# Scores of four heads in one group in the last steps of a causal attention

## The chip, the cores and the metric

The kernel runs on one core of one Trainium2 chip. The metric is the device time of one execution in microseconds (us), the median over several runs. A profiled execution was taken beside them; its rows are what the text quotes.

## The reference

Three blocks in a row: a half-weighted mixture-of-experts layer, an attention, and the same expert layer again, each on layer-normalised rows. x has 4 sequences of 2048 rows with 256 columns. Cut to the attention, which alone is touched (16 heads of 16 columns):

```python
q = (x @ Wq)...; k = (x @ Wk)...; v = (x @ Wv)...
node_probs = jax.nn.softmax((x @ Wr)..., axis=-1)
...
q_r = q * cos_w + rotate_half(q) * sin_w
k_r = k * cos_w + rotate_half(k) * sin_w
node_w = jnp.einsum('bhik,bhjk->bhij', node_probs, node_probs)
scores = jnp.einsum('bhid,bhjd->bhij', q_r, k_r) * SCALE
scores = scores + jnp.log(node_w + 1e-08)
scores = jnp.where(causal[None, None], scores, -jnp.inf)
attn = jax.nn.softmax(scores, axis=-1)
out = jnp.einsum('bhij,bhjd->bhid', attn, v)
return out.transpose(0, 2, 1, 3).reshape(B, S, E) @ Wo
```

## The kernel before

**Three stages.** `experts` runs twice, before and after `attention`, each with its own pools of SBUF and PSUM. The second call begins when the pools of the attention have been given back.

**Units and steps.** The attention works on units: one sequence and one group of four heads, 16 units in all. Within a unit the queries are cut into four blocks of 512 (`ib`), and for each block the keys are gone through in pieces of 128 rows (`at`, listed in `turns`). One such piece is a step: 36 in a unit, 576 in all. A step is 512 queries wide; the pieces on the diagonal are packed, so that the step "two" consists of a piece of 384 and one of 128 columns, and the step "one" is 256 wide. Each head occupies one strip of 32 partitions of the tiles qT and kT, so a matmul of one head uses one 32-row strip of the TensorE array.

**What a step does.** For each head, `scores` (L1037) multiplies a kT piece with the qT block into one PSUM bank; `weights` takes exp of it on ScalarE into an SBUF tile `ex`, and on masked pieces GpSimd cuts off what lies above the diagonal; `summed` (L1063) multiplies ex with the values into the accumulators acc[0] and acc[1] (one for each half of the four nodes), and `summed_weights` (L1080) into den.

**Maxima.** The scores of a block need the maximum of each query row first. `maximum` (L1104) computes the scores the other way round, queries by keys, for two heads into two PSUM banks, and VectorE reduces them. When all of a block are there, `negated` turns them (a ps_t transpose, L1130) and adds them to qT. This work is kept in two lists, `left[0]` and `left[1]` (one for each pair of heads), and `take` issues one entry. The maxima run ahead of the steps that need them: `ask` issues those of the very first block at once, and during the first unit the loop takes additional ones. So the lists run out before the steps do.

**The order of instructions** is written out by hand in `run`: nothing reorders the queues. For each step it goes through two phases, `pair` 0 and 1. A phase issues the scores of the *next* step for one pair of heads, one entry of maxima for the other pair of heads (`take(1 - pair, width)`), the exps of that pair of the next step, and then one half of the sums of the current step. So while maxima are left, two scores and two maxima, on four different strips, stand one after the other on TensorE; afterwards the two scores stand there alone. Behind each phase side work is put in: generators for preparing the next unit, for `normalise` (ps_o transposes, L1146) and `project` (ps_p transposes, L1192; ScalarE copy to oc; ps_w matmuls, L1202). At the last step of a block ScalarE also copies acc[0] (after phase 0), acc[1] and den (after phase 1) out of PSUM.

**PSUM.** Of the eight banks, acc[0], acc[1] and den hold three. `bank(name, tag)` hands out the others in two rings: tag "sc" with two banks, for scores, and tag "mx" with three, for maxima and for all side work (ps_o, ps_p, ps_w, ps_t).

```python
BANKS = {"sc": 2, "mx": 3}
...
return ps_rg.tile([P, 512], F32, name=name, tag=tag, bufs=BANKS[tag])
```

All operations of VectorE, ScalarE and GpSimd in the attention pass through a recording helper, so the profile shows them under its line, L78. Names tell them apart: ex<-sc is the exp of a score, top<-mx the reduction of a maximum. TensorE's weight loads are listed as an engine of their own, PEld. An fp32 matmul leaves two records.

Of the kernel before, what the change touches and what calls it, by code (L numbers as in the profile page):

```python
# [94 lines left out]
def macaron_kernel(  # L95
# [487 lines left out]
    def attention():  # L583
# [43 lines left out]
        def bank(name, tag="mx"):  # L627
            if not gaps["steps"]:
                tag = turn_of.pop(0)
                turn_of.append(tag)  # L630
            return ps_rg.tile([P, 512], F32, name=name, tag=tag, bufs=BANKS[tag])
# [374 lines left out]
        def pieces(ib, at):  # L1006
            if at == "two":
                return [(4 * ib + 1, P, 3 * P, 0), (4 * ib + 3, 3 * P, P, 3 * P)]
            if at == "one":
                return [(4 * ib + 2, 2 * P, 2 * P, 0)]  # L1010
            return [(at, 0, 512, 0)]

        def columns(at):
            return 256 if at == "one" else 512
# [10 lines left out]
                return t[:, of[0] : of[0] + P].unsqueeze(1)  # L1025
            return t.rearrange("p (n w) -> p n w", w=P)[:, of[0] // P : of[1] // P + 1 : 3, :]

        def scores(u, ib, at, pair):

            q = u["qT"][ib]  # L1030
            out = [bank("sc", "sc") for _ in range(2)]
            for jt, off, n, to in pieces(ib, at):
                k = u["kT"][jt // 4]
                js = slice((jt % 4) * P, (jt % 4 + 1) * P)
                for j in range(2):
                    r = slice(32 * (2 * pair + j), 32 * (2 * pair + j) + 32)
                    nc.tensor.matmul(  # L1037
                        out[j][:, to : to + n], lhsT=k[r, js], rhs=q[r, off : off + n],
                        start=True, stop=True,
                    )  # L1040
            return out

        def weights(tiles, u, ib, at, pair):
            n = columns(at)
            for j in range(2):
                ex = pool.tile([P, 512], F32, name="ex", tag="ex", bufs=8)
                act.activation(ex[:, 0:n], tiles[j][:, 0:n], AF.Exp, scale=D**-0.5)
                cut = masked(ib, at)
                if cut:
                    diag = blocks(ex, cut)  # L1050
                    gps.affine_select(
                        out=diag, in_=diag, pattern=[[0, len(cut)], [1, P]],
                        compare_op=ALU.is_ge, fill=0.0, base=0, channel_multiplier=-1,
                    )
                u["ex"][2 * pair + j] = ex
# [168 lines left out]
        def maxima(ib):  # L1224

            wide = [(i, c) for c in range(ib) for i in range(4)]
            heavy = ["two", (3, ib)]
            if not wide:
                return [(at, at) for at in heavy[:1] + ["one"] + heavy[1:]]
            order = [o for at, w in zip(heavy, (0, 2)) for o in ((at, wide[w]), (wide[w], at))]  # L1230
            order += [(wide[1], wide[1]), (wide[3], wide[3])]
            return order + [("one", "one")] + [(at, at) for at in wide[4:]]

        left = {
            pair: [(u, ib, at) for u in units for ib in range(NI) for at in maxima(ib)]
            for pair in range(2)
        }
# [98 lines left out]
        def begin(phase):  # L1336
            nonlocal begun
            if begun < len(units):
                w = units[begun]
                behind.append(prepare(w))  # L1340
                due.append([phase, STEPS[w["g"] == 0], w])
                begun += 1
# [9 lines left out]
        def onward(force=False):  # L1352

            w = due[0]
            took = advance(behind, force)
            parted()
            if not took and [g.__name__ for g in behind[:2]] == ["quarter"] * 2:
                took = advance(behind, False, 1)
            w[1] -= took is True
            if w[2]["ready"]:  # L1360
                due.pop(0)
            return took

        def pace(phase):

            if due:
                for _ in range(max(1, -(-due[0][1] // max(1, due[0][0] - phase)))):
                    if not due or not onward(phase > due[0][0]):
                        break
# [4 lines left out]
        while units[0]["blocks"] < NI:  # L1374
# [6 lines left out]
            at = min(some, key=lambda at: max(known.get(id(behind[at]), (0, [0.0]))[1]))  # L1381
# [7 lines left out]
        def order(u, behind):  # L1389

            while u["shared"] and u["queued"] < min(NI, 1 + behind):
                urgent.append(weighted(u, 4 * u["queued"]))
                u["queued"] += 1

        def run():
            for n, (u, ib, at) in enumerate(steps):
                if n == 0:
                    begin(span // 2)
                if ib == NI - 1 and at == turns[ib][0]:

                    begin(2 * n + span - 8)
                if n == 0:
                    for pair in range(2):
                        weights(scores(u, ib, at, pair), u, ib, at, pair)
                ex = dict(u["ex"])
                order(u, NI)
                while len(u["vn"]) <= max(jt for jt, _, _, _ in pieces(ib, at)) // 4:
                    advance(urgent, True)
                nxt = steps[n + 1] if n + 1 < len(steps) else None
                width = columns(nxt[2]) if nxt is not None else 512  # L1410
                if nxt is not None and nxt[2] == turns[nxt[1]][0]:
                    while nxt[0]["blocks"] <= nxt[1]:
                        onward(True)
                    ask(nxt[0], nxt[1])
                last = at == turns[ib][-1]
                for pair in range(2):
                    gaps["free"] = True
                    clock.now = max(clock.now, vec.end - LAG, act.end - LAG)
                    clock.now += 1.07 * width / 512
                    if nxt is not None:  # L1420
                        made = scores(*nxt, pair)
                    take(1 - pair, width)
                    if u is units[0] and ib > 0 and n % 2 and pair:
                        take(0)
                        take(1)
                    if nxt is not None:
                        weights(made, *nxt, pair)
                    summed(u, ib, at, pair, ex)
                    summed_weights(u, ib, at, ex, pair)
                    clock.now += 1.5 * columns(at) / 512  # L1430
                    if pair == 0:
                        if last:
                            while held:
                                advance(urgent, True)
                            got = [
                                pool.tile([P, 512], F32, name="oT", tag="oT", bufs=3)
                                for _ in range(3)
                            ]
                            act.copy(got[0], acc[0])
                        pass  # L1440
                    else:
                        if last:
                            act.copy(got[1], acc[1])
                            act.copy(got[2], den)
                            if u["g"] == 0:
                                outs[u["b"], ib] = pool.tile([P, 4, E], F32, name="o", tag="o", bufs=5)
                            held.append((id(u), ib))
                            urgent.append(normalise(u, ib, got))
                            if u["g"] == NG - 1:
                                urgent.append(project(u["b"], ib))  # L1450
                    if pair == 1 and ib == NI - 1:
                        after = units.index(u) + 1
                        if after < len(units):
                            order(units[after], sum(
                                turns[ib].index(at) >= max(
                                    m for m, o in enumerate(turns[ib])
                                    if any(jt // 4 == b for jt, _, _, _ in pieces(ib, o))
                                )
                                for b in range(NI)
                            ))  # L1460
                    if not advance(first):
                        advance(urgent)
                    pace(2 * n + pair)
            gaps["free"] = True
            while advance(urgent, True):
                pass

        with tc.manual_schedule():
            run()
# [45 lines left out]
```

## Time and profile before

| What | us |
|---|---|
| Median of 3 timed runs | 4581.84 |
| Lowest and highest of them | 4573.15, 4585.91 |
| Profiled execution | 4589.68 |
| Span of its records | 4588.0 |
| Mean granted TensorE clock | 0.932 |
| First expert stage and start of the attention, 0 to 700: TensorE busy | 471.82 |
| Attention, 3800 to 4000: TensorE busy | 198.20 of 200.00 |
| Attention without maxima, 4066.15 to 4160.15: TensorE busy | 94.00 of 94.00 |
| End of the attention, 4160.15 to 4182.78: TensorE busy | 10.46 of 22.63 |
| Second expert stage, 4182.78 to 4588.0: TensorE busy | 252.36 of 405.22 |

How to read the profile: one execution on the chip, times in microseconds from the start of the span. Each row names the engine, the line of the kernel, the operation, and the tiles as out<-in, with partitions x elements. Matmuls are pipelined and their ends are modelled, so two rows on TensorE may overlap; the distance from the start of one group to the start of the next is the better measure of what a group costs. In a row of the timeline, the number after the opening bracket is the engine's idle time before it, and behind the arrow stands what ended it.

### The profile page before, as it was taken

The page shows a single profiled execution, that of the slowest core. Times are in us where ns is not written, and L with a number is a line of the kernel's source. Part 1 is how long each engine was busy: PE and PEld are TensorE (multiplying, and loading weights), DVE is VectorE, ACT ScalarE, POOL GpSimd, SP SyncE. Part 2 cuts the span into 40 slices and gives each one's busy share as a digit, 9 for nine tenths or more (in the row PEclk, how much of TensorE's full clock was granted, in tenths as well). Part 3 has the DMA queues.
Part 4 walks back from the last instruction along what each step waited for, and adds up shares of the span by engine and source line. Part 5 has one row for each costly group of instructions (what it writes and reads, how often), then busy time and mean ns, then how long its engine had stood idle before and what let it go on. Part 6 is the DMA issues. An engine that isn't in the chain of part 4 may idle for free. (4 is left out here: it accounts for less than half of the span.)

```text
span 4588.0 us, 89695 instructions
## 1 busy us (share of the span) xinstructions
PE 4118.6 (90%) x36512; PEld 1841.0 (40%) x36512; DVE 2957.4 (64%) x7855; ACT 1907.3 (42%) x3671; POOL 1644.3 (36%) x2482
## 2 busy tenths in 40 slices
PE   5575598999999999999989999999999999997376
PEld 2354333434344434443434443444444444332254
DVE  6852666667755667676667776767576767523771
ACT  4133132444454445455434454454344444444122
POOL 4285322243324333342233342413242424202177
PEclk8686688999999999999999999999999999998588
DMA  7244000000000000001000000010000000004144
GB/s 251 66 81 89 1 1 1 1 1 1 20 29 20 17 13 1 1 1 38 15 15 29 1 1 1 1 38 15 29 15 1 1 1 2 1 29 147 60 73 75
DMA packets 108046, 136.27 MB, mean 30 GB/s; under 512 B 7792, under 2 KB 102256, under 8 KB 106480
## 3 DMA queue, kind: packets, MB, share of 16 engines
q1 hardware_dynamic: 81152, 95.84, 6.4%
q0 software_dynamic: 24576, 33.57, 4.5%
q8 instruction: 286, 4.69, 0.4%
q10 hardware_dynamic: 1904, 1.13, 0.1%
q14 instruction: 128, 1.05, 0.1%
HBM read 77.03 MB, written 61.87 MB: 30 GB/s over the span
## 5 line engine op out<-in xcount | busy, mean ns | idle before, releaser
L78 ACT ACTIVATE ex<-sc 128x512 f32<-128x512 f32 (+1 forms) x2304 | 1197.7, 572 | 1579.5 <-PE mx L1104 1342.1
L1104 PE MATMUL mx<-kT,qT 32*128 32x512 f32 (+3 forms) x5120 | 1355.1, 581 | 10.3 <-DVE top L78 9.6
L78 DVE TENSOR_REDUCE top<-mx 128x1 f32<-128x512 f32 x1536 | 1003.1, 684 | 490.5 <-PE mx L1104 485.5
L1037 PE MATMUL sc<-qT,kT 32*128 32x512 f32 (+3 forms) x5120 | 1297.3, 576 | 12.8 <-ACT ex L78 9.2
L1063 PE MATMUL acc<-ex,vn 128*32 128x512 f32 (+3 forms) x10240 | 1188.7, 544 | 0.0
L78 POOL TENSOR_SCALAR_AFFINE_SELECT ex<-ex 128x128 f32<-128x128 f32 (+1 forms) x768 | 255.3, 338 | 1348.2 <-ACT ex L78 1337.9
L78 DVE CUSTOM_DVE_ANT_0 mx<-mx,edge 128x384 f32<-128x384 f32 (+3 forms) x1024 | 498.9, 503 | 315.5 <-PE mx L1104 248.9
L1080 PE MATMUL den<-ex,share 128*4 128x256 f32 (+1 forms) x9216 | 677.9, 370 | 0.0
L1037 PEld LDWEIGHTS sc<-qT,kT 32*128 32x128 f32 x5120 | 430.2, 185 | 417.3 <-ACT ex L78 216.1
L1063 PEld LDWEIGHTS acc<-ex,vn 128*32 128x32 f32 x10240 | 216.4, 108 | 778.0 <-issue 708.2
L1104 PEld LDWEIGHTS mx<-kT,qT 32*128 32x128 f32 x5120 | 452.5, 187 | 84.2 <-DVE top L78 73.7
L1080 PEld LDWEIGHTS den<-ex,share 128*4 128x4 f32 x9216 | 248.7, 88 | 579.4 <-issue 551.3
L78 POOL TENSOR_TENSOR by_node<-by_node 128x512 f32<-128x512 f32 x64 | 86.3, 1349 | 555.1 <-DVE by_node L78 555.0
L439 DVE TENSOR_SCALAR at<-row_b,low_t 128x128 bf16<-128x128 bf16 x1024 | 174.4, 286 | 57.0 <-PE ps_l L442 57.0
L482 POOL DMA_INDIRECT xg<-normed,where x128 | 130.2, 1017 | 207.0 <-DVE sc L461 168.6
L78 POOL TENSOR_TENSOR vn<-v,share 128x1024 f32<-128x1024 f32 x64 | 125.9, 1973 | 194.2 <-PE acc L1063 192.8
L501 ACT COPY xT<-ps_t 128x512 f32<-128x512 f32 x64 | 37.5, 586 | 303.0 <-PE ps_t L498 302.8
L530 PE MATMUL ps_o<-w,hT 128*128 128x256 f32 x512 | 147.3, 448 | 0.0
L78 DVE DVE_READ_ACCUMULATOR2_ANT top<- 128x1 f32 x1024 | 144.9, 141 | 0.0
L724 PEld LDWEIGHTS ps_a<-wa,xnT 128*128 128x128 f32 x1024 | 127.2, 202 | 27.5 <-issue 14.1
L724 PE MATMUL ps_a<-wa,xnT 128*128 128x80 f32 x1024 | 136.7, 289 | 0.0
L78 DVE TENSOR_TENSOR by_node<-ps_o,tot 128x512 f32<-128x512 f32 x128 | 88.0, 690 | 74.8 <-PE ps_o L1146 61.6
(218 smaller groups left out, 4788.8 us busy)
## 6 DMA issues: line engine op xcount, KB each, us to landing
xs<-x SPq DMA_DIRECT2D x32, 512.0 KB, 5.6
normed<-xn SPq DMA_DIRECT2D x32, 512.0 KB, 3.3
xs<-x SPq DMA_DIRECT2D x64, 256.0 KB, 2.7
w<-w SPq DMA_DIRECT2D x4, 2048.0 KB, 9.6
xs_o<-x SPq DMA_DIRECT2D x16, 512.0 KB, 3.9
x<-xs_o SPq DMA_DIRECT2D x16, 512.0 KB, 3.0
out<-xs_o SPq DMA_DIRECT2D x16, 512.0 KB, 4.1
xg<-normed,where POOLq DMA_INDIRECT x128, 2.7
```

What stands on the lines that cost most here:

```text
L78: return getattr(self.engine, name)(*args, **kw)
L439: nc.vector.tensor_scalar(at[:, t, :], row_b, low_t[:, c + t, e : e + 1], None, ALU.is_equal)
L482: inst = nc.gpsimd.indirect_dma_start(out=xg, out_offset=None, in_=normed, in_offset=bass.IndirectOffsetOnAxis(ap=lists[e][0][:, i : i + 1 ...
L501: nc.scalar.copy(xT[:, :, i * P : (i + 2) * P], ps)
L530: nc.tensor.matmul(po[:, j, :], lhsT=hT[:, f, at : at + P], rhs=w2[:, f, e, :], start=f == 0, stop=f == 1,)
L724: nc.tensor.matmul(ps[:, j, :], lhsT=u["xnT"][:, c, (t + j) * P : (t + j + 1) * P], rhs=wa[:, c, u["g"], cols], start=c == 0, stop=c == 1,)
L1037: nc.tensor.matmul(out[j][:, to : to + n], lhsT=k[r, js], rhs=q[r, off : off + n], start=True, stop=True,)
L1063: nc.tensor.matmul(acc[half][32 * h : 32 * h + 32, off : off + n], lhsT=u["vn"][jt // 4][:, jt % 4, h, 32 * half : 32 * half + 32], rhs=ex ...
L1080: nc.tensor.matmul(den[32 * h : 32 * h + K, off + a - to : off + z - to], lhsT=u["share"][:, jt, h, :], rhs=ex[h][:, a:z], start=at == tur ...
L1104: nc.tensor.matmul(made[j][:, to : to + n], lhsT=q[r, i * P : (i + 1) * P], rhs=u["kT"][c][r, 0:n], start=True, stop=True,)
```

## The change

In the steps in which no maximum is left in either list, the scores of both pairs of the next step are issued together in phase 0, four heads in a row; the third and fourth get banks of the ring "mx". The exps stay where they were: those of the first pair in phase 0, those of the second in phase 1. As long as maxima are left, nothing is changed.

```diff
-        def scores(u, ib, at, pair):
+        def scores(u, ib, at, *pairs):
 
             q = u["qT"][ib]
-            out = [bank("sc", "sc") for _ in range(2)]
+            heads = [2 * pair + j for pair in pairs for j in range(2)]
+            out = [bank("sc", tag) for tag in ("sc", "mx")[: len(pairs)] for _ in range(2)]
             for jt, off, n, to in pieces(ib, at):
                 k = u["kT"][jt // 4]
                 js = slice((jt % 4) * P, (jt % 4 + 1) * P)
-                for j in range(2):
-                    r = slice(32 * (2 * pair + j), 32 * (2 * pair + j) + 32)
+                for j, h in enumerate(heads):
+                    r = slice(32 * h, 32 * h + 32)
                     nc.tensor.matmul(
...
                 last = at == turns[ib][-1]
+
+                four = nxt is not None and not any(left.values())
                 for pair in range(2):
                     gaps["free"] = True
                     clock.now = max(clock.now, vec.end - LAG, act.end - LAG)
                     clock.now += 1.07 * width / 512
-                    if nxt is not None:
+                    if four and pair == 0:
+                        made = scores(*nxt, 0, 1)
+                    elif four:
+                        made = made[2:]
+                    elif nxt is not None:
                         made = scores(*nxt, pair)
                     take(1 - pair, width)
```

## The prediction

> **What bounds the kernel now.** First the page: which engine is full, and where.
>
> ```profile
> PE 4118.6 (90%) x36512; PEld 1841.0 (40%) x36512; DVE 2957.4 (64%) x7855; ACT 1907.3 (42%) x3671; POOL 1644.3 (36%) x2482
> PE   5575598999999999999989999999999999997376
> PEclk8686688999999999999999999999999999998588
> ```
>
> TensorE is 90% busy, and full in all of attention (slices 8 to 36 of 40; one slice is 114.7 us). At its busiest there is no other engine to blame: what shortens PE's work there shortens the run. Next the share of each engine in windows near the end of attention (columns: window, length, then busy us of PE, PEld, DVE, ACT, POOL, granted clock, DMA share, GB/s).
>
> ```profile
> 3800.00:4000.00 200.00, 198.20 (x2004) 73.33 (x1995) 136.20 (x322) 86.05 (x166) 69.55 (x121) 1.00 0.01 2
> 4066.15:4160.15 94.00, 94.00 (x772) 33.52 (x772) 6.02 (x13) 38.32 (x74) 7.07 (x18) 1.00 0.11 35
> ```
>
> The second window is the stretch without maxima: the last maximum matmul starts at 4064.2 by the rows of tile mx, and VectorE falls from 68% to 6%. PE stays at 94.00 of 94.00 at a granted clock of 1.00, ACT is busy 38.32. So PE bounds this stretch too, and only this stretch is edited. Third, the order of time on PE on both sides of that border (start, length, engine, line, operation):
>
> ```profile
> 4055.57 0.70 PE L1037 MATMUL sc<-qT,kT 32*128 32x512 f32 x2
> 4055.59 0.70 PE L1104 MATMUL mx<-kT,qT 32*128 32x512 f32 x2
> 4056.11 0.59 PE L1037 MATMUL sc<-qT,kT 32*128 32x512 f32 x2
> 4056.12 0.59 PE L1104 MATMUL mx<-kT,qT 32*128 32x512 f32 x2
> 4056.64 1.07 PE L1063 MATMUL acc<-ex,vn 128*32 128x512 f32 x8
> 4057.53 0.61 PE L1080 MATMUL den<-ex,share 128*4 128x256 f32 x8
> 4058.07 0.70 PE L1037 MATMUL sc<-qT,kT 32*128 32x512 f32 x2
> ...
> 4066.15 1.13 PE L1037 MATMUL sc<-qT,kT 32*128 32x512 f32 x4
> 4067.21 1.06 PE L1063 MATMUL acc<-ex,vn 128*32 128x512 f32 x8
> 4068.09 0.61 PE L1080 MATMUL den<-ex,share 128*4 128x256 f32 x8
> 4068.64 1.13 PE L1037 MATMUL sc<-qT,kT 32*128 32x512 f32 x4
> ```
>
> Each fp32 matmul leaves two records, so "x4" is two heads. Above the dots, two scores and two maxima, which use the other two 32-row strips of the array, run from 4055.57 to 4056.64: 1.07 us for four. Below, two scores alone run from 4066.15 to 4067.21: 1.06 us for two. A pair costs what four cost. acc then takes 0.88 (4067.21 to 4068.09), den 0.55; a phase is 2.49, a step of two phases 4.98.
>
> **The change, part by part.** In the changed program's PE order, the two score pairs of 17 steps have become one group of four, put where the first pair stood; no other instruction moves on PE, and the orders on DVE, ACT, POOL and SP are the same. The 17 are 14 steps of 512 columns, one in two pieces (384 and 128) and two of 256, all of the steps that start after 4066.15.
>
> Removed: 17 separate second pairs. A 512-wide pair is 1.06; the two-piece pair lasts from 4116.78 to 4117.84, 1.06; a 256-wide one from 4071.71 to 4072.34, 0.63. If the group of four costs what a pair costs, 15 x 1.06 + 2 x 0.63 = 17.2 us leave PE. How long four scores in a row last, no row shows: two of them always stood alone or beside maxima. Bounds: 1.06 (all strips at once) to 2.12 (one pair after the other, which is no gain). I take 1.06, because the row of two scores and two maxima has the same shape, the same four strips and four PSUM banks, and differs only in which operand is stationary.
>
> The Trainium skill, page "TensorE: Matmul & The Clock Gate", section "Measured speedup vs the span model", speaks against so full a gain: it lists four row tiles of K=32, N=512 at 3.07 times, not 4. By it, as an estimate, the group would last 4/3.07 = 1.30 pairs and the run would gain about 11 us instead. The trace's 1.07 against 1.06 does not agree with that figure, and the measurement decides.
>
> Added: waits for PSUM. Heads 3 and 4 now sit in the three mx banks until their exps are done, and these stand in ACT's queue behind whatever was put there between the phases. One ordinary step after the change is 1.06 + 2 x (0.88 + 0.55) = 3.92 us on PE. ACT begins 0.10 after the group's end (4101.75 to 4101.85) and takes 0.54 for an exp (1.08 for two): all four end at 1.06 + 0.10 + 2.16 = 3.32, so every bank is free 0.60 us before the next group wants it. VectorE, idle 94% here, frees the ps_o, ps_w and ps_t tiles that share the mx banks within a phase. The cover is ACT's slack; it is gone at three places, where a copy stands between the exps:
>
> ```profile
> 4079.81 1.36 PE L1037 MATMUL sc<-qT,kT 32*128 32x512 f32 x4
> 4081.66 1.56 PE L1037 MATMUL sc<-qT,kT 32*128 32x512 f32 x4
> ...
> 4084.58 0.65 PE L1192 MATMUL ps_p<-cst,o 128*128 128x128 f32 x4
> 4085.27 0.59 ACT L78 COPY oc<-ps_p 128x512 f32<-128x512 f32 x1 [1.26 <-PE ps_p L1192]
> ```
>
> (a) Twice a ps_p transpose (L1192) comes after the first phase, and its ACT copy waits for it: 1.06 + 1.43 + 0.59 + 0.10 + 0.59 = 3.77, then two exps to 4.85. PE, which also did the 0.59 of ps_p, wants the banks at 4.51. With 0.08 for the release (an estimate: the exps that end at 4082.05 and the scores behind them, done at 4083.15, leave 0.04 beyond 1.06): 0.42 each, 0.84 for both. Behind the waiting score stands all of PE's queue. (b) Once, where ib goes from 2 to 3, the step is short (256 columns: 1.06 + 0.45 + 0.55 + 0.45 = 2.51 on PE) and the copy of acc[0] (0.59) stands between the exps; the third ends at 1.06 + 0.10 + 1.08 + 0.59 + 0.54 = 3.37, with the release 3.45: a wait of 0.94. Together 1.78. In the rows above the kernel already waits there: 4079.81 to 4081.09 is 0.22 over 1.06, 4081.66 to 4083.15 is 0.43 over, together 0.65, which goes. Net added: 1.1, between -0.65 (no wait left) and, if each wait is twice that, 2.9.
>
> Sum: 17.2 - 1.1 = 16.1 us off the stretch of 94.00.
>
> What lies behind it moves up whole: the last normalise and project run from 4160.15, the last output transfer is issued at 4178.57, and VectorE's first instruction of the second expert stage starts at 4182.78, put down to that transfer; the loads of xs start at 4182.71. Nothing of that stage runs earlier, so no cover is lost and no queue other than PE's changes. Clock grants in that stage (mean 0.77) may fall otherwise by a few us either way; that is in the spread below.
>
> The profiled span 4588.0 (its run: 4589.68) becomes 4571.9. The profiled run is 0.17% above the median of the timed runs, 4581.84; the same 16.1 off the median gives 4565.7.
>
> **Rivals.**
> 1. *Four scores stretch each other.* All four read the same kT tile as weights and the same qT tile as moving data, where the maxima swap the two. For: no row shows four in a row. Against: a pair that shares both tiles lasts no longer than two scores and two maxima that don't. Midway between its bounds (1.59 a group) 8 of the 17 us stay: 4582 - 17.2/2 + 1.1 = 4574. The page named above would have it here, on this side of the middle.
> 2. *They don't overlap at all* (or the group waits each time about as long as a pair lasts): 4582 to 4583.
> 3. *Slower: the mx banks come back late in every step.* The place is the third and fourth score of each group, whose banks are held by the exps behind ACT's queue. It decides from a wait of 1.06 per step on, that is, with the last exp ending 4.98 after the group began, not 3.32. With 1.5 us in each, 17 x 1.5 - 17.2 = 8 us are lost: 4590. For: three banks for two heads and all side work, and a copy in the queue has this effect at three places. Against: ACT is busy 38.32 of 94.00, and sits idle 1.40 us before each ordinary pair of exps. The Trainium skill, page "TensorEngine Tiling (Array Packing)", section "PSUM Bottleneck", warns of just this: tiling quickens TensorE but not the emptying of PSUM. The trace agrees in kind only at the three places counted.
> 4. *The change does not act*: excluded but for its size, by the 17 groups in the order.
>
> **How the numbers follow.** Forecast 0.82, rival 1 0.07, rival 2 0.06, rival 3 0.05. The likeliest gives 4565.7. What a measurement here can tell from no change is about 0.3%, 13.7 us (the three runs lie 12.8 apart). The forecast clears that by little: I give it 9 in 10. Faster: 0.82 x 0.9 + 0.01 of rival 1 = 0.75; same: 0.08 + 0.06 + 0.06 = 0.20; slower 0.05. Range: the forecast's own bounds are gains of 17.8 (no wait left) and 14.3 (doubled waits), 4564 to 4567.5; a median of few runs may lie off by about half of those 12.8; and rival 1 belongs in. 4554 to 4580 leaves out part of the scatter, rival 2's upper half and rival 3.
>
> **What would show it.** In the profile after, PE's groups "sc x8" (four heads) should last 1.06 to 1.1 at 512 columns, be followed by acc, den, acc, den without scores between, every 3.9 us; the stretch without maxima should last 77 to 79 us; the waits of 0.4, 0.4 and 0.9 should stand before or inside the scores that follow the two ps_p copies and the ib change. Groups of 1.4 or more would mean rival 1 or 2; sc waiting for ex in most steps, rival 3; a short stretch with an unchanged total would mean that the second expert stage took the gain back.

## The result and the profile after

| | Kernel before | Changed kernel |
|---|---|---|
| Median of 7 runs, us | 4581.78 | 4566.78 |
| Lowest and highest | 4573.15, 4585.91 | 4562.16, 4567.21 |
| Ratio of the runs, 95% interval | | 0.9966, 0.9954 to 0.9978 |
| Span of the profiled execution | 4588.0 | 4563.0 |

The changed kernel is faster by 15.0 us between the medians; the interval allows 10 to 21. The two profiled spans differ by 25.0, more than that. Cut at the same instructions in both traces, this is where the 25.0 lie:

| Part of the span | Before | After | Gain |
|---|---|---|---|
| Up to the first scores without maxima (same order of instructions) | 4066.15 | 4061.72 | 4.4 |
| From there to the last den of the attention | 94.32 | 75.99 | 18.3 |
| From there to VectorE's first instruction of the second expert stage | 22.31 | 22.06 | 0.3 |
| Second expert stage (same order of instructions) | 405.22 | 403.23 | 2.0 |

Only the second row is the change's. The first and the last part hold nothing that was edited; the section on the experiments shows how far they scatter.

The page of the changed kernel, the same three lines as in the prediction: busy time, TensorE's busy slices, granted clock.

```profile
PE 4100.1 (90%) x36512; PEld 1831.8 (40%) x36512; DVE 2957.7 (65%) x7855; ACT 1903.5 (42%) x3671; POOL 1641.9 (36%) x2482
...
PE   5585698999999999999989999999899999997386
...
PEclk8687698999999999999999999999999999998588
```

TensorE is busy 18.5 us less with the same number of instructions: what went is time, not work. Next the window without maxima, cut at its last den (columns as before):

```profile
4061.72:4137.71 75.99, 75.99 (x777) 29.28 (x777) 6.03 (x13) 36.54 (x74) 7.04 (x18) 1.00 0.13 43
```

PE is still full (75.99 of 75.99), at the same clock of 1.00, and ACT is at 36.54: PE still bounds the stretch. Busy time here includes a wait inside a group of scores, so the waits are read from the starts. The order of time of PE, and behind the first ps_p transpose of ACT too:

```profile
4061.72 1.14 PE L1038 MATMUL sc<-qT,kT 32*128 32x512 f32 x8
4062.80 1.07 PE L1064 MATMUL acc<-ex,vn 128*32 128x512 f32 x8
4063.68 0.61 PE L1081 MATMUL den<-ex,share 128*4 128x256 f32 x8
4064.11 1.04 PE L1064 MATMUL acc<-ex,vn 128*32 128x512 f32 x8
4064.97 0.61 PE L1081 MATMUL den<-ex,share 128*4 128x256 f32 x8
4065.51 0.66 PE L1131 MATMUL ps_t<-cst,slot_m 128*128 128x128 f32 x4
...
4073.89 1.89 PE L1038 MATMUL sc<-qT,kT 32*128 32x512 f32 x8
4075.71 1.06 PE L1064 MATMUL acc<-ex,vn 128*32 128x512 f32 x8
...
4077.14 0.66 PE L1193 MATMUL ps_p<-cst,o 128*128 128x128 f32 x4
...
4077.83 0.58 ACT L78 COPY oc<-ps_p 128x512 f32<-128x512 f32 x1 [0.78 <-PE ps_p L1193]
4078.31 1.09 ACT L78 ACTIVATE ex<-sc 128x512 f32<-128x512 f32 x2
...
4079.15 1.14 PE L1038 MATMUL sc<-qT,kT 32*128 32x512 f32 x8
4080.22 1.06 PE L1064 MATMUL acc<-ex,vn 128*32 128x512 f32 x8
```

"sc x8" is four heads. The first group lasts from 4061.72 to 4062.80, 1.07 to 1.08 us, as the pair did. The den that acc follows at once takes 0.43 (4063.68 to 4064.11), the one ahead of the ps_t transposes 0.54 (4064.97 to 4065.51). At the change of ib the group takes 1.82 (4073.89 to 4075.71), so it waits 0.75. The weight loads of this group show whose wait it is, six for the first three heads and, after an exp, two for the fourth:

```profile
4073.89 0.31 PEld L1038 LDWEIGHTS sc<-qT,kT 32*128 32x128 f32 x6 [0.41 <-ACT ex L78]
4074.66 0.29 PEld L1038 LDWEIGHTS sc<-qT,kT 32*128 32x128 f32 x2 [0.47 <-ACT ex L78]
```

Behind the ps_p copy, the exps of the second pair end at 4079.40, after the next group's start at 4079.15; still that group lasts 1.07 and waits for nothing.

### The profile page after: what moved, and what is told of

Same layout as the page of the kernel before. It is cut to its first block, busy times and chain, and to the rows that moved or that the text cites. A ratio compares the mean times of both kernels' runs of the same rounds, so it can differ in the third digit from the quotient of the medians.

```text
span 4563.0 us, 89704 instructions
## 1 busy us (share of the span) xinstructions
PE 4100.1 (90%) x36512; PEld 1831.8 (40%) x36512; DVE 2957.7 (65%) x7855; ACT 1903.5 (42%) x3671; POOL 1641.9 (36%) x2482
## 3 DMA queue, kind: packets, MB, share of 16 engines
q14 instruction: 129, 1.06, 0.1%
## 5 line engine op out<-in xcount | busy, mean ns | idle before, releaser
L1038 PE MATMUL sc<-qT,kT 32*128 32x512 f32 (+3 forms) x5120 | 1278.5, 575 | 12.9 <-ACT ex L78 9.2
L78 POOL TENSOR_TENSOR prod<-turn,node 128x512 f32<-128x512 f32 x64 | 74.3, 1167 | 168.4 <-ACT turn L78 168.4
```

What stands on the lines that cost most here:

```text
L78: return getattr(self.engine, name)(*args, **kw)
L1038: nc.tensor.matmul(out[j][:, to : to + n], lhsT=k[r, js], rhs=q[r, off : off + n], start=True, stop=True,)
```

## The experiments

All are measured on one stretch: from the first scores without maxima to VectorE's first instruction of the second expert stage. Its first part, up to the last den, is PE's alone; the second part, the last transposes, transfers and their landing, scatters between 21.8 and 22.4 us with no edit in it that would explain it.

| Kernel | Starts at | To the last den | Whole stretch | Ratio to before, 95% interval |
|---|---|---|---|---|
| Before | 4066.15 | 94.32 | 116.63 | |
| Changed | 4061.72 | 75.99 | 98.05 | 0.9966, 0.9954 to 0.9978 |
| Two strips only | 4064.24 | 88.75 | 111.14 | 0.9981, 0.9972 to 0.9991 |
| Banks only | 4063.99 | 93.66 | 116.00 | 0.9998, 0.9988 to 1.0007 |
| Last eight steps | 4061.70 | 85.42 | 107.19 | 0.9978, 0.9968 to 0.9988 |
| Side work late | 4058.11 | 75.16 | 97.54 | single run, 4563.19 us |
| Banks exchanged | 4053.95 | 77.10 | 99.49 | single run, 4559.56 us |
| Side work and copy late | 4057.32 | 74.69 | 96.54 | 0.9960, 0.9946 to 0.9974 |

The second column is the scatter of the rest: all eight programs put the same work in the same order on every engine up to that point, and reach it between 4053.95 and 4066.15. This is why gains of a few us are read from the stretch.

**Two strips only.** Are four strips of the array at work at once, or does only the place of the scores in the queue matter? This kernel leaves out the scores of the second pair of heads in the grouped steps; those of the first pair stand there twice.

```diff
                 for j, h in enumerate(heads):
-                    r = slice(32 * h, 32 * h + 32)
+                    g = h if len(heads) == 2 else h % 2
+                    r = slice(32 * g, 32 * g + 32)
```

> In the 17 steps without maxima the third and fourth score matmul use the strips of the first and second (heads 2 and 3 of these steps get the scores of heads 0 and 1, so the output is wrong there); place in the queue, number of matmuls, PSUM banks and waits are those of the changed kernel. Measure: the stretch from the first score after the last maximum to VectorE's first instruction of the second expert stage, 116.63 us before and 98.05 after the change. Theory (the gain is that four strips work at once): a 512-wide group takes 2.1 and not 1.07 us, the stretch is 114 to 115.5 us, the time 0.9 to 3 us below the kernel before. Rival (the gain comes from the place, the fewer changes between kinds of matmul and the added banks): the groups stay near 1.1 us, the stretch at 98 to 100, the ratio at 0.9966.

The order of time on PE in this kernel, one ordinary group and what follows it:

```profile
4130.36 1.99 PE L1039 MATMUL sc<-qT,kT 32*128 32x512 f32 x8
4132.28 1.06 PE L1065 MATMUL acc<-ex,vn 128*32 128x512 f32 x8
```

The group takes 1.92 (4130.36 to 4132.28): the strips do count, and the rival, that the groups would stay near 1.1, falls. But it isn't the 2.1 of the theory. Two pairs in a row cost 0.20 less than two pairs apart, in the 256-wide groups as well (1.07 against 2 x 0.63), and the stretch is 111.1, not 114 to 115.5; the median lies 8.8 us below that of the kernel before in the runs beside it, not 0.9 to 3, but its interval begins at 4 and holds the 5.5 of the stretch. If each visit to the scores has one fixed cost and each pair adds the same time, a separate pair of 1.06 is 0.86 (1.92 - 1.06) for the scores and 0.20 for leaving acc and den and returning to them; this split is an estimate from the two figures. Both theories were half right: of the 18.3 us, the two strips more bring 88.75 - 75.99 = 12.8 net; the rest, 5.6, comes without them.

**Banks only.** The pairs stay apart, the second one in mx banks.

```diff
-        def scores(u, ib, at, *pairs):
+        def scores(u, ib, at, *pairs, tags=("sc", "mx")):
...
-            out = [bank("sc", tag) for tag in ("sc", "mx")[: len(pairs)] for _ in range(2)]
+            out = [bank("sc", tag) for tag in tags[: len(pairs)] for _ in range(2)]
...
-                    if four and pair == 0:
-                        made = scores(*nxt, 0, 1)
-                    elif four:
-                        made = made[2:]
+                    if four:
+                        made = scores(*nxt, pair, tags=("sc", "mx")[pair:])
```

> The two pairs stay apart as in the kernel before, but the second pair of the 17 steps sits in mx banks. Same stretch (116.63 before, 98.05 after). Theory: banks alone bring only the end of the waits at the change of ib, 0.2 to 0.7 us: 115.9 to 116.6, ratio 0.999 to 1.001. Rival (the kernel before was held by its two sc banks): 98 to 105, ratio near 0.997.

The change of ib on PE in this kernel:

```profile
4077.65 1.13 PE L1038 MATMUL sc<-qT,kT 32*128 32x512 f32 x4
4078.70 0.64 PE L1064 MATMUL acc<-ex,vn 128*32 128x256 f32 x8
4079.27 1.13 PE L1038 MATMUL sc<-qT,kT 32*128 32x512 f32 x4
4080.33 1.08 PE L1064 MATMUL acc<-ex,vn 128*32 128x512 f32 x8
```

The stretch is 116.00, as the theory had it. To the last den it is 0.66 shorter than before, and that is the two waits at the change of ib (0.22 and 0.43): there the two pairs now last 1.05 and 1.06. The sc ring held this stretch nowhere else.

**Last eight steps.** Groups only from the ninth step before the end on.

```diff
-                four = nxt is not None and not any(left.values())
+                four = nxt is not None and not any(left.values()) and n >= len(steps) - 9
```

> Groups of four only in the last 8 of the 17 steps. Theory (each grouped step gains on its own): 7 x 1.06 + 0.63 for the pairs and 7 x 0.14 for den followed at once by acc make 9.0 us, so the stretch is 107.6 us and the ratio about 0.998. Rival (most of it is gained around the border of the maxima and the change of ib, which come earlier than these 8 steps): a gain of under 5 us, stretch over 111.

To the last den 8.90 us less than before, 9.0 expected. These eight steps gain what the theory gives them, so the gain does not come from the border of the maxima or the change of ib.

**Side work late.** Nothing between den of the first phase and acc of the second, in any of the 17 steps.

```diff
-                    if not advance(first):
-                        advance(urgent)
+                    for _ in range((2 if pair else 0) if four else 1):
+                        if not advance(first):
+                            advance(urgent)
```

> The changed kernel with the side work of the 17 steps put after phase 1 only, so that acc follows den at once in all of them and not in 11. Theory (a change between kinds of matmul, from den to scores or transposes, costs 0.11 to 0.14 us, and the grouping leaves out 11 of them): 6 more are saved, 0.8 us; the stretch goes from 98.05 to 97.2 us, and each den before acc takes 0.43 us up to the start of acc where it takes 0.54 before a transpose. Rival (den is short there for another reason, such as how ends are modelled): the stretch stays at 98.0 within 0.2.

A step with side work in this kernel, on PE:

```profile
4077.35 0.61 PE L1081 MATMUL den<-ex,share 128*4 128x256 f32 x8
4077.78 1.04 PE L1064 MATMUL acc<-ex,vn 128*32 128x512 f32 x8
4078.64 0.61 PE L1081 MATMUL den<-ex,share 128*4 128x256 f32 x8
4079.19 0.48 PE L1203 MATMUL ps_w<-wo,oc 128*128 128x256 f32 x1
```

The same den takes 0.43 ahead of acc (4077.35 to 4077.78) and 0.55 ahead of ps_w (4078.64 to 4079.19). To the last den the kernel saves 0.83 us, 0.8 expected, which is what six such changes of about 0.14 come to. In the whole stretch 0.51 of it is left (97.54, where 97.2 was said), within the scatter of its second part.

**Banks exchanged.** Why did the two waits behind the ps_p copies not come?

```diff
-            out = [bank("sc", tag) for tag in ("sc", "mx")[: len(pairs)] for _ in range(2)]
+            out = [bank("sc", tag) for tag in (("mx", "sc") if len(pairs) > 1 else ("sc",)) for _ in range(2)]
```

> The changed kernel with the banks exchanged: the first pair of a group in the mx ring, the second in the two sc banks. Now the fourth score needs the bank of the very last exp, as the prediction had taken it for all three waits. Theory (the two waits of 0.42 us behind the ps_p copies did not come because the fourth score got the bank of the first and not of the second exp of the pair): they come now, 0.3 to 0.4 us each, the wait at the change of ib grows from 0.76 to about 1.3, and the stretch from 98.05 to 99.1 to 99.4 us. Rival (the exps give banks back earlier than their rows end, so no such wait exists): 98.0 within 0.2 apart from the change of ib.

PE and ACT around the change of ib and behind the first ps_p copy:

```profile
4066.11 2.38 PE L1038 MATMUL sc<-qT,kT 32*128 32x512 f32 x8
...
4068.43 1.06 PE L1064 MATMUL acc<-ex,vn 128*32 128x512 f32 x8
...
4071.03 1.09 ACT L78 ACTIVATE ex<-sc 128x512 f32<-128x512 f32 x2
...
4071.87 1.43 PE L1038 MATMUL sc<-qT,kT 32*128 32x512 f32 x8
...
4073.22 1.07 PE L1064 MATMUL acc<-ex,vn 128*32 128x512 f32 x8
```

Now the waits are there: 1.25 at the change of ib (2.32 - 1.07), 0.28 behind this copy (4071.87 to 4073.22 is 1.35) and 0.35 behind the other. The exps end at 4072.12, and 1.10 later the group is done: the bank comes back with the end of the exp's row. So in the changed kernel, where the group behind this copy ended only 0.82 after the second exp (4079.40 to 4080.22), the fourth score cannot have needed that exp's bank. The two programs as built agree: in the changed kernel, behind both copies, the third score gets the bank of ps_p and the fourth the bank of the third score before it; here the fourth gets the bank of the fourth. To the last den this kernel is 1.11 longer than the changed one; the whole stretch, 99.49, is a little over the 99.1 to 99.4 that were expected.

**Side work and copy late.** The kernel with late side work, and the copy of acc[0] behind the exps of the second pair:

```diff
-                            act.copy(got[0], acc[0])
-                        pass
+                            if not four:
+                                act.copy(got[0], acc[0])
...
                         if last:
+                            if four:
+                                act.copy(got[0], acc[0])
                             act.copy(got[1], acc[1])
```

> The kernel with late side work, and the copy of acc[0] at the change of ib put behind the exps of the second pair. Theory: the wait of 0.76 us there falls to 0.2 to 0.5 us, and with the late side work the stretch is 96.6 to 97.0 us; the time is that of the changed kernel less 1 us, ratio about 0.9964, not to be told from 0.9966. Rival (the copy is then late for the next sums into acc[0], which wait instead): the stretch is 97.2 or more.

The change of ib on PE in this kernel:

```profile
4069.49 1.40 PE L1038 MATMUL sc<-qT,kT 32*128 32x512 f32 x8
4070.83 1.06 PE L1064 MATMUL acc<-ex,vn 128*32 128x512 f32 x8
```

The group takes 1.34 there, so the wait is 0.27, and acc starts right behind it: no new wait for the copy. It is the shortest stretch of all, 96.54, 1.5 us under the changed kernel's and slightly under what was expected. Its ratio of 0.9960 lies inside the interval of the changed kernel's, so the stretch is better and the time can't be told apart.

## Why the prediction was right

The mechanism was right and the total came close: 4565.7 forecast, 4566.78 measured. In the stretch 16.1 us were forecast and 18.3 found to its last den; two terms of the sum were off. By its steps:

- *PE bounds the stretch before and after.* Right: 94.00 of 94.00 before, 75.99 of 75.99 after.
- *A group of four costs what a pair costs.* Right in size: 1.07 against 1.06, and 0.64 against 0.63 at 256 columns. The row of two scores and two maxima was a good stand-in for four scores; rivals 1 and 2 are out. The page "TensorE: Matmul & The Clock Gate" of the Trainium skill (section "Measured speedup vs the span model"), from whose 3.07 the prediction estimated 1.30 pairs for the group, does not carry over so: 1.07/1.06 is 1.01. The page's table gives a speedup of four tiles, where the estimate counted in pairs of two; no run here has the scores one at a time, so the 3.07 itself stays untested.
- *17.2 us leave with the pairs.* The sum is right, its reading was too simple. The prediction took the 1.06 of a pair as work of the strips. In the kernel on two strips 0.20 of it goes as soon as the pair stands behind another. Of the 17.2, about 15 x 0.85 + 2 x 0.42 = 13.6 is the strips' (1.92 - 1.07 and 1.06 - 0.64 in each group), 17 x 0.20 = 3.4 comes from the fewer changes, and 0.2 did not leave, since a group lasts 0.01 longer than a pair.
- *den 0.55, whatever follows.* This term was mis-sized: where acc follows at once den takes 0.43, and that acc 0.86 instead of 0.88, about 0.14 in 11 steps, 1.5 us that the sum did not have. The rows stood in the trace of before, at the end of the attention, where den is followed by acc (4159.60 to 4160.03 is 0.43):

```profile
4159.60 0.61 PE L1080 MATMUL den<-ex,share 128*4 128x256 f32 x8
4160.03 0.61 PE L1063 MATMUL acc<-ex,vn 128*32 128x256 f32 x8
```

- *Waits: 0.42, 0.42 and 0.94.* The step that failed is the place "two exps to 4.85": the prediction let the fourth score wait for the second exp behind each ps_p copy. It came to 0, 0 and 0.75. The exps ended as worked out (4079.40 - 4075.71 is 3.69 from the first acc, and 4.85 - 1.06 is 3.79), but the bank that the fourth score got was the one of the exp before it, free 0.5 earlier: the mx ring does not hand its banks out in a fixed round, which this step of the prediction needs. With the banks exchanged the waits are there, at 0.28 and 0.35. The 0.08 for the release was also too much: the row that it names gives 0.04, and with the banks exchanged it is 0.03 (1.10 from the end of the exp to the end of the group, less 1.07).
- *Rival 3, a wait in every step* (the Trainium skill, page "TensorEngine Tiling (Array Packing)", section "PSUM Bottleneck"): out. ACT is busy 36.54 of 75.99, and one wait of 0.75 is all. In the ordinary step from 4118.87 the four exps end at 4122.09 (4120.03 + 2.06), 0.57 before the next group starts.
- *The rest moves up whole.* Right: from the last den to VectorE's first instruction of the second expert stage 22.31 and 22.06, and that stage 405.22 and 403.23.

Together: 13.6 for the strips, 3.4 and 1.5 for fewer changes, 0.65 for the two old waits, less 0.75 for the new one, is 18.4; the traces have 18.3. The prediction's 16.1 is 2.2 short of the stretch: the 1.5 of den and the 1.0 of waits that did not come (1.78 - 0.75) lie on the same side, and both are small against the 17.2. That the medians differ by only 15.0, nearer to 16.1 than to 18.3, is luck: their interval of 10 to 21 holds both.

## What to carry to other kernels

Where small matmuls that use different strips of the array stand apart in the queue, put them side by side: here a second pair of heads cost nothing more than 0.01 us beside the first one. Price a group from the start of one to the start of the next, and ask what part of that is its neighbours: the same den took 0.43 or 0.54 by what came behind it. And when something new is put into a ring of banks that is shared, work out which release each taker really waits for; a wait that is computed for the last holder may not exist.

## What was not expected of the hardware

- Going from sums to scores and back costs TensorE time of its own: by the estimate above 0.20 us for each additional visit to a pair of scores (2 x 1.06 - 1.92), and 0.11 to 0.12 for den before scores or transposes instead of acc (0.54 to 0.55 against 0.43). The Trainium skill, page "TensorEngine Tiling (Array Packing)", section "Key Properties", states that a change of tiling mode, not of the tile alone, drains TensorE; scores use strips of rows and the sums strips of columns, and the numbers above agree with it. What inside the array takes the time no run here shows.
- Up to the first scores without maxima, eight profiled executions of the same work differ by 12.2 us, more than most of the edits of this study.
